# Two layers on one core: how the last sparsification's steps are spread among the closing products' additions

## Chip, core and metric

The kernel runs on one core of a Trainium2 chip. The metric is the device time of one execution in microseconds (us). Of three runs before the change the median is 1851.51 us (1851.51 to 1860.42).

## What is computed

The reference is a model of two layers on 2 x 1024 rows of 512 numbers in float32. Layer 0 is a scan branch with a small MLP beside a gated feed-forward network with a Hadamard transform; layer 1 is attention beside a gated feed-forward network whose hidden values are thinned: of each group of four, only the two of greatest magnitude stay. The part that matters here is the last one:

```
def _sparsify_2to4(h):
    g = h.reshape(B, S, I // 4, 4)
    a = jnp.abs(g)
    _, idx = jax.lax.top_k(a, 2)
    pos = jnp.arange(4)
    mask = (pos == idx[..., 0:1]) | (pos == idx[..., 1:2])
    return (g * mask).reshape(B, S, I)
h = silu(x @ w_gate) * (x @ w_up)          # 512 -> 2048
return _sparsify_2to4(h) @ w_down          # 2048 -> 512
...
x = x + attention(xn) + ffn(xn)
```

## The kernel before, in words

The engines work through one program in four stages: layer 0, attention, then layer 1's feed-forward network in the pool `c`. That last stage is what this study is about. It has 16 units: two pairs of row blocks (512 rows each), four groups of 512 hidden columns, two halves of a group. One unit makes 2 x 128 hidden columns for two row blocks in `gate_up`, with the matrix products of L179 by a Strassen-like scheme of seven products in place of eight. Two units fill `hs[n]`, the hidden values of group n (n from 0 to 7): 128 partitions, four members of each group of four, two row blocks i, 512 rows.

Each group is then thinned and multiplied by its rows of the down projection:

- `sparsify(n, half)` (L1385 to L1414) is a generator with twelve steps for one half of the rows (256 of each block). Step 1 is the absolute value on ScalarE (L1399, into `ab`); the other eleven are on VectorE: the smaller and larger of pairs (L1400, L1404), comparisons (L1402, L1403, L1406, L1407), the sums that turn them into a count of wins (L1408 to L1410), and two products of a mask with `h`, in place (L1414). Its buffers `ab`, `lo`, `first`, `both` and `way` exist once, so the second half's absolute value must wait until the first half has read `ab` for the last time (L1407). `some_steps(n, half, count)` runs the next `count` steps.
- `down_by_seven` (L246) makes the down projection of a half in seven products of 128 x 256 (L297), which it adds to the residual `x1` on VectorE (L310), or leaves to GpSimd (L315). Its products lie in two PSUM banks in turn; a product may begin on a bank only when the one before has been read from it.
- `row_down(n, i, j)` (L1449) makes 128 rows of the down projection directly: four matmul calls of 128 x 512 (L1454), which the profile counts as eight instructions, then an addition to the residual on VectorE (L1459), and for the last group of a pair of blocks the store of these rows by SyncE (L1462). It takes its bank from three pairs in turn.

While a unit's gate-and-up products run, hooks inside `gate_up` insert steps of the group before. Behind the last unit no gate-and-up products are left. What stands there is the list `tail`: the remaining products of group 6, first half (five of L297, with GpSimd's addition), the four `row_down` of group 6's second half, the thinning of group 7 and its eight `row_down`. The list is built by hand before the loop and then run through; `in_program_order(start2)` fixes the order on TensorE, VectorE, ScalarE and GpSimd as it is issued. Each engine works through its own queue in that order, and semaphores hold an instruction until what it reads or overwrites is ready.

Before the change the list interleaves as follows: the first half's absolute value; then, for each of the five products of group 6, a `row_down` of group 6 and one step, the product and one step (the fifth product has no `row_down` ahead of it); then two more steps (the two L1414 of the first half) and the second half's absolute value; then four `row_down` of group 7's first half, with 3, 3, 3 and 2 steps of the second half behind their additions; then the four `row_down` of the second half. A step behind a product stands on VectorE's queue behind that product's addition.

Of the kernel before, what the change touches and what calls it, by code (L numbers as in the profile page):

```python
# [35 lines left out]
def two_layers(ctx: ExitStack, tc: tile.TileContext, t: dict, out: bass.AP):  # L36
# [307 lines left out]
    with tc.tile_pool(name="a", bufs=1) as a:  # L344
# [386 lines left out]
        def down_weights(n, m):  # L731
# [16 lines left out]
        hidden_first, hidden_last, down, products_of = down_by_seven(  # L748
            a, h0, td, quarters_w, lambda n: n // (NU // 2) * 2, in_place=True
        )  # L750
# [35 lines left out]
        for q, n in enumerate(((0, 2), (0, 4), (1, 2), (1, 4))):  # L786
            put0(*n, fwht_rows, q)
            for m in range(4):
                n, at = (0, (4, 5, 6, 6)[m]) if q == 0 else divmod(4 * q + 3 + m, 7)
# [11 lines left out]
        for base in (0, NU):  # L801
            i, d = 2 * base // NU, base + (1 if base else 3)
# [88 lines left out]
        n, second_half = NU - 1, list(products_of(NU - 1, 1))  # L891
# [14 lines left out]
    with tc.tile_pool(name="b", bufs=1, reuse_waits="tile") as b:  # L906
# [304 lines left out]
        for u in range(len(units)):  # L1211

            for half in range(2):
                n = per * u - ahead + (3, 11)[half]
# [11 lines left out]
            for j in range(2):  # L1226
                n = per * u + 8 * j + 7
# [93 lines left out]
        n = len(second)  # L1321
# [14 lines left out]
    with tc.tile_pool(name="c", bufs=1, reuse_waits="tile") as c_:  # L1336
# [81 lines left out]
        def some_steps(n, half, count):  # L1418
# [5 lines left out]
        hidden_first, hidden_last, down, products_of = down_by_seven(  # L1424
            c_, hs, td, quarters_w, lambda n: 2 * units[2 * n][0]
        )
# [9 lines left out]
        between1, tail = {}, []  # L1436
# [5 lines left out]
        def sequence(n, half):  # L1442

            for step in products_of(n, half):
                yield step
                if step[0] == down and step[3] > 4:
                    yield store, n, half, step[3] - 5
# [16 lines left out]
        for n in range(groups - 1):  # L1464
# [8 lines left out]
            for half, at in enumerate(((8, 11),) if end else (range(4, 11), range(11, 18))):  # L1473
                steps = list(sequence(n, half))
# [11 lines left out]
                put1(u, 10, hidden_last, n, 1)  # L1486


        n = groups - 1
        rows = [(row_down, n - 1, i, j) for j in (2, 3) for i in range(2)]  # L1490
        behind_last, tail = tail, [(some_steps, n, 0, 1)]
        for what in behind_last:
            if what[0] == down:
                if rows:
                    tail += [rows.pop(0), (some_steps, n, 0, 1)]
                tail += [what, (some_steps, n, 0, 1)]
            else:
                tail.append(what)
        tail += [(some_steps, n, 0, 2), (some_steps, n, 1, 1)]
        for half in range(2):  # L1500
            for j in (2 * half, 2 * half + 1):
                for i in range(2):
                    tail.append((row_down, n, i, j))
                    if half == 0:
                        tail.append((some_steps, n, 1, (3, 3, 3, 2)[2 * j + i]))

        tt, next_tt, second = None, None, None
        s_of = {}
# [117 lines left out]
```

## Time and profile before

| What | us |
|---|---|
| median of three runs | 1851.51 |
| the profiled execution's own time | 1851.87 |
| its span, first to last instruction | 1850.1 |
| TensorE (PE) busy | 1794.7 (97%) |
| VectorE (DVE) busy | 1124.7 (61%) |
| GpSimd (POOL) busy | 819.6 (44%) |
| ScalarE (ACT) busy | 478.5 (26%) |
| mean granted clock of TensorE | 0.996 |

In the profile PE is TensorE's matrix work and PEld its weight loads, which overlap it. L1454 is line 1454 of the kernel. "PE dr L1454 x8" are eight instructions that write tile `dr`; "DVE h L1414" is VectorE's step that writes `h`. "A <- B" means that A waited for B. The granted clock is the share of full speed that TensorE was given. All times within the span are counted from its first instruction. The last gate-and-up product ends at 1786.4 us; the tail is what follows, some 64 us.

How VectorE's queue stands in a part of the tail before (start, length, engine, line, instruction; in brackets the idle time ahead and what ended it):

```profile
1806.91 0.69 DVE L1459 TENSOR_TENSOR x<-x,dr 128x512 f32<-128x512 f32 x1 [2.15 <-PE dr L1454]
1807.52 0.42 DVE L1408 TENSOR_TENSOR way<-both 128x512 bf16<-128x512 bf16 x1
1808.71 0.69 DVE L310 TENSOR_TENSOR x<-x,d 128x512 f32<-128x512 f32 x1 [0.77 <-PE d L297]
1809.31 0.68 DVE L1409 TENSOR_TENSOR first<-first,way 128x1024 bf16<-128x1024 bf16 x1
```

### The profile page before, as it was taken

What the parts mean: (1) busy time and instruction counts of PE and PEld (TensorE: products, weight loads), DVE (VectorE), ACT (ScalarE), POOL (GpSimd) and SP (SyncE); (2) the same over time, 40 slices, a digit from 0 to 9 for tenths busy, and PEclk for the clock granted to TensorE, in tenths of its full rate; (3) what the DMA queues carried; (4) which work ended last, traced back from release to release, by engine and by line L of the source; (5) the groups of instructions that cost most, each with busy time, mean ns of one, the idle gap of its engine ahead of it and who ended that gap; (6) DMA issues with size and microseconds to landing.
All of it is one profiled execution on the core that took longest, in us unless ns stands there. A gap on an engine that the chain in (4) does not pass through costs nothing.

```text
span 1850.1 us, 18897 instructions
## 1 busy us (share of the span) xinstructions
PE 1794.7 (97%) x7348; PEld 916.4 (50%) x7348; DVE 1124.7 (61%) x1464; ACT 478.5 (26%) x683; POOL 819.6 (44%) x711
## 2 busy tenths in 40 slices
PE   7999999999999999999999999999999999999998
PEld 4446566555555564333333333333455555555553
DVE  3685444556544438566666566752867778668654
ACT  2322222222221102334343443412212212211210
POOL 4335364256542222467666766623243343334300
PEclk9999999999999999999999999999999999999999
DMA  6121111011101100000001000011011112201101
GB/s 228 35 80 34 35 35 46 23 46 35 35 23 34 35 18 12 1 12 13 12 1 35 12 13 1 24 46 42 27 57 34 46 32 72 80 23 57 34 1 46
DMA packets 29465, 68.12 MB, mean 37 GB/s; under 512 B 3392, under 2 KB 11584, under 8 KB 27840
## 3 DMA queue, kind: packets, MB, share of 16 engines
q1 hardware_dynamic: 28656, 66.61, 11.1%
q8 instruction: 59, 0.97, 0.2%
q10 hardware_dynamic: 720, 0.30, 0.1%
q14 instruction: 30, 0.25, 0.0%
HBM read 62.70 MB, written 4.19 MB: 36 GB/s over the span
## 4 chain that ended last, share of the span: by engine, by line
PE 87%; DVE 5%; POOL 3%; ACT 2%; issue 2%; DMA 0%; SPq 0%; ACTq 0%; POOLq 0%; DVEq 0%
PE p_a L179 20%; PE p_c L179 19%; PE d L297 19%; PE pq L990 6%; PE m L1042 4%; PE s L1095 4%; PE o L1137 3%; PE po L990 3%; PE pv L990 3%; PE dr L1454 2%; POOL acc L1145 2%; PE w L1157 1%; DVE tops L1050 1%; PE pp L579 1%; PE s L1101 1%
## 5 line engine op out<-in xcount | busy, mean ns | idle before, releaser
L315 POOL TENSOR_TENSOR x<-x,de 128x512 f32<-128x512 f32 x87 | 125.4, 1456 | 297.3 <-DVE x L310 162.5
L1145 POOL TENSOR_TENSOR acc<-acc,pt 128x1024 f32<-128x1024 f32 (+3 forms) x138 | 233.6, 1717 | 0.0
L1050 DVE TENSOR_REDUCE tops<-m 128x2 f32<-128x1024 f32 (+2 forms) x192 | 180.8, 955 | 49.1 <-PE m L1042 44.6
L310 DVE TENSOR_TENSOR x<-x,d 128x512 f32<-128x512 f32 x145 | 99.2, 684 | 151.5 <-PE d L297 150.5
L1112 ACT ACTIVATE pt<-s 128x1024 f32<-128x1024 f32 (+3 forms) x160 | 115.1, 766 | 180.1 <-PE s L1101 166.9
L297 PE MATMUL d<-td,h 128*128 128x256 f32 x592 | 139.9, 380 | 2.2 <-DVE h L272 2.2
L297 PEld LDWEIGHTS d<-td,h 128*128 128x128 f32 x592 | 112.2, 190 | 46.2 <-issue 29.2
L990 PE MATMUL pq<-xt,wqk 128*128 128x512 f32 x256 | 124.5, 614 | 0.8 <-ACT qk L1006 0.8
L179 PE MATMUL p_a<-t_a,s_a 128*128 128x512 f32 x256 | 116.9, 600 | 2.0 <-DVE t_a L156 2.0
L179 PE MATMUL p_c<-xt,s_c 128*128 128x512 f32 x256 | 115.2, 593 | 2.5 <-DVE e_c L224 1.4
L179 PE MATMUL p_a<-xt,w 128*128 128x512 f32 x256 | 116.8, 599 | 0.7 <-ACT xt L136 0.7
L179 PE MATMUL p_a<-xt,s_a 128*128 128x512 f32 x256 | 116.6, 598 | 0.0
L179 PE MATMUL p_c<-xt,gu 128*128 128x512 f32 x256 | 114.9, 592 | 0.0
L179 PE MATMUL p_c<-t_c,s_c 128*128 128x512 f32 x256 | 114.6, 592 | 0.0
L1049 DVE TENSOR_TENSOR m<-m,mask 128x256 f32<-128x256 f32 x128 | 54.7, 427 | 97.3 <-PE m L1042 92.7
L1042 PE MATMUL m<-qk,qk 32*128 32x512 f32 (+3 forms) x768 | 107.2, 533 | 3.7 <-ACT acc L1112 3.0
L1095 PE MATMUL s<-qk,qk 32*128 32x512 f32 (+3 forms) x768 | 93.5, 532 | 3.1 <-ACT pt L1112 2.2
L172 POOL TENSOR_TENSOR s_c<-gu,s_c 128x512 f32<-128x512 f32 x16 | 20.4, 1275 | 134.2 <-PE p_c L179 134.2
L1117 POOL TENSOR_SCALAR_AFFINE_SELECT pt<-pt 128x256 f32<-128x256 f32 x112 | 48.3, 448 | 69.5 <-ACT pt L1112 68.9
L990 PEld LDWEIGHTS pq<-xt,wqk 128*128 128x128 f32 x256 | 44.2, 189 | 65.9 <-issue 61.8
L179 PEld LDWEIGHTS p_a<-xt,s_a 128*128 128x128 f32 x256 | 47.2, 190 | 57.1 <-issue 56.7
L179 PEld LDWEIGHTS p_c<-xt,s_c 128*128 128x128 f32 x256 | 48.5, 190 | 54.2 <-issue 52.9
(240 smaller groups left out, 3044.6 us busy)
## 6 DMA issues: line engine op xcount, KB each, us to landing
w<-in_W SPq DMA_DIRECT2D x32, 512.0 KB, 3.6
gu<-in_gu SPq DMA_DIRECT2D x32, 512.0 KB, 3.5
wd<-in_down SPq DMA_DIRECT2D x8, 1024.0 KB, 4.8
x<-in_x SPq DMA_DIRECT2D x16, 256.0 KB, 4.3
w2h<-in_W2q SPq DMA_DIRECT2D x4, 1024.0 KB, 11.5
xr<-in_x SPq DMA_DIRECT2D x16, 256.0 KB, 2.7
wqk<-in_WqkvT SPq DMA_DIRECT2D x16, 256.0 KB, 3.1
out_x<-x SPq DMA_DIRECT2D x16, 256.0 KB, 2.0
```

Source lines behind the costliest of these rows:

```text
L179: nc.tensor.matmul(pair[:, m, :], a[:, m, k, :], x[:, k, :], start=start and k == 0, stop=stop and k == 1, skip_group_check=True,)
L297: nc.tensor.matmul(out_[:, j, :], lhs[:, q, j * P : (j + 1) * P], rhs[:, q], start=m in (0, 1, 3, 4) and j == q == 0, stop=j == q == 1, sk ...
L310: nc.vector.tensor_add(r, r, out_)
L315: nc.gpsimd.tensor_add(r, r, u2[half])
L990: nc.tensor.matmul(got[0], lhs(k), rhs(k), start=(k == 0), stop=(k == KC - 1))
L1042: nc.tensor.matmul(pair[h // 2][:, h % 2, :e], q[rows, qt * P : (qt + 1) * P], k[rows, c * 512 : c * 512 + e], start=True, stop=True,)
L1049: nc.vector.tensor_add(d, d, mask.unsqueeze(1).to_broadcast([P, 2, P]))
L1050: nc.vector.tensor_reduce(out=tops[u][:, c, qt, 2 * p : 2 * p + 2], in_=pair[p][:, :, :e], axis=mybir.AxisListType.X, op=ALU.max,)
L1095: nc.tensor.matmul(pair[h // 2][:, h % 2, s:], k[rows, kt * P : (kt + 1) * P], q[rows, cols], start=True, stop=False,)
L1112: nc.scalar.activation(pt[:, :, s:], pair[p][:, :, s:], AF.Exp, scale=1.0 / math.sqrt(HD))
L1137: nc.tensor.matmul(po[rows, s:], v[:, rows], pts[h // 2][:, h % 2, s:], start=(kt == 0), stop=last, tile_position=(0, h * HD),)
L1145: eng.tensor_add(acc[:, :, s:], acc[:, :, s:], pt[:, :, s:])
```

## The change

It replaces the one-step interleaving by a written-out list. `steps` has twelve entries, each a tuple of (half, count); `go_on` takes the next entry and appends those steps to the tail. One entry is taken before the first product, one behind each of the nine products of group 6 (four `row_down`, five of L297), and one behind each of group 7's first two `row_down`. On VectorE that gives, by addition: first half's L1400 ahead of the first addition; then behind the additions in turn L1402; L1403 and L1404; L1406 and L1407; L1408 to L1410; both L1414; the second half's L1400; L1402; L1403 and L1404; L1406 and L1407; and behind the first two additions of group 7 L1408 and L1409; L1410 and both L1414. On ScalarE the second half's absolute value is issued behind the first half's L1410. No instruction is added or dropped, and the order on TensorE, GpSimd and SyncE is the same.

```diff
         n = groups - 1
         rows = [(row_down, n - 1, i, j) for j in (2, 3) for i in range(2)]
-        behind_last, tail = tail, [(some_steps, n, 0, 1)]
+        steps = [
+            ((0, 2),), ((0, 1),), ((0, 2),), ((0, 2),), ((0, 3), (1, 1)), ((0, 2),), ((1, 1),),
+            ((1, 1),), ((1, 2),), ((1, 2),), ((1, 2),), ((1, 3),),
+        ]
+
+        def go_on():
+            for half, count in steps.pop(0) if steps else ():
+                tail.append((some_steps, n, half, count))
+
+        behind_last, tail = tail, []
+        go_on()
         for what in behind_last:
+            if what[0] == down and rows:
+                tail.append(rows.pop(0))
+                go_on()
+            tail.append(what)
             if what[0] == down:
-                if rows:
-                    tail += [rows.pop(0), (some_steps, n, 0, 1)]
-                tail += [what, (some_steps, n, 0, 1)]
-            else:
-                tail.append(what)
-        tail += [(some_steps, n, 0, 2), (some_steps, n, 1, 1)]
+                go_on()
         for half in range(2):
             for j in (2 * half, 2 * half + 1):
                 for i in range(2):
                     tail.append((row_down, n, i, j))
-                    if half == 0:
-                        tail.append((some_steps, n, 1, (3, 3, 3, 2)[2 * j + i]))
+                    go_on()
```

## The prediction

> **What bounds the kernel now.** I read the page first, then the chain of waits in order of time for the last 85 us (the change touches only what follows the last gate-and-up unit of layer 1), then busy time and granted clock by stretches there, then VectorE's own timeline, and last the order in which the changed kernel puts the instructions on each engine. By the page TensorE is busy 97% of the span and carries 87% of the chain that ended last, so a gain must come from a place where TensorE stands still or runs slowly. The end of the chain (start in us, length, what):
>
> ```profile
> 1803.44 3.43 PE dr L1454 x8
> 1806.87 3.47 PE d L297 x16
> 1810.34 0.03 issue
> 1810.37 0.02 DVEq L310
> 1810.39 0.04 issue
> 1810.44 0.69 DVE x L310
> 1811.12 0.60 DVE first L1410
> 1811.72 1.15 DVE h L1414
> 1812.87 0.04 issue
> 1812.91 15.71 PE dr L1454 x32
> 1828.63 0.02 issue
> 1828.65 0.69 DVE x L1459
> 1829.34 1.15 DVE h L1414
> 1830.48 0.04 issue
> 1830.53 15.71 PE dr L1454 x32
> 1846.24 0.02 issue
> 1846.26 0.69 DVE x L1459
> ```
>
> TensorE leaves the chain twice, each time for VectorE's last steps of a sparsification: from 1810.34 to 1812.91 (2.57 us) and from 1828.63 to 1830.53 (1.90). The first row shows what one row product, eight matrix instructions, costs undisturbed: 3.43. Thirty-two should then take 13.72, and both groups take 15.71. The granted clock shows most of the other 1.99 (stretch, its length, busy time and count of PE, PEld, DVE, ACT and POOL, clock, DMA share, GB/s):
>
> ```profile
> 1812.90:1814.00 1.10, 1.08 (x3) 0.61 (x4) 1.09 (x1) 0.00 (x0) 0.00 (x0) 0.95 0.00 0
> 1814.00:1817.20 3.20, 3.20 (x5) 1.20 (x4) 0.00 (x0) 0.00 (x0) 0.00 (x0) 0.50 0.00 0
> 1817.20:1828.60 11.40, 11.40 (x27) 4.78 (x25) 9.34 (x12) 0.00 (x0) 0.00 (x0) 1.00 0.18 69
> 1830.50:1834.40 3.90, 3.87 (x5) 1.65 (x6) 1.11 (x1) 0.00 (x0) 0.00 (x0) 0.56 0.13 43
> 1834.40:1846.30 11.90, 11.82 (x28) 4.94 (x26) 2.10 (x4) 0.00 (x0) 0.00 (x0) 1.00 0.18 66
> ```
>
> After each stop TensorE runs some 3.3 us at half clock. That loses 0.06 + 1.60 = 1.66 behind the first stop and 3.90 x 0.44 = 1.72 behind the second. The rest, about 0.27, is the restart: the first row product behind the 1.31 us gap at 1787.69 takes 3.70 where 3.43 is usual, with the clock at 1.00.
>
> **The change part by part.** No instruction is added or taken away on any engine, and TensorE's order is the same. What moves is the place of VectorE's 22 sparsification instructions among the additions, and ScalarE's second absolute value.
>
> What goes: both stops with what hangs on them. From 1810.34 to 1846.24 is 35.90 us; eight row products at 3.43 are 27.46 with nothing in between. The difference is 8.44: 4.47 of standing, 3.98 of restart and half clock. For it TensorE must find everything ready eight times, so I replayed VectorE in the new order. It takes its queue in order. The pitches are from this trace's neighbouring starts: an addition 0.60 (1818.35 to 1818.95), each of L1400 to L1404 1.14 (1818.95, 1820.09, 1821.22), L1406 and L1407 0.60, L1408 0.45, L1409 and L1410 0.60, the two L1414 together 2.35. An addition can't start before its product ends, by the present chain at 1791.39, 1793.12, 1796.55, 1798.28, 1801.71, 1803.44, 1806.87, 1808.60 and 1810.34.
>
> First half: L1400 starts at 1791.0, when ScalarE's first absolute value ends (1790.97), ahead of the first addition, which moves from 1791.43 to 1792.15. Then L1402 1792.75, addition 1793.9, L1403 1794.5, L1404 1795.7, addition 1796.9, L1406 1797.5, L1407 1798.1, addition 1798.7, L1408 1799.3, L1409, L1410 to 1800.9, addition 1801.75, both L1414 from 1802.35 to 1804.7. The half is thin at 1804.7, where TensorE needs it at 1810.34: 5.6 us early, not 2.57 late.
>
> Second half: its absolute value reuses the first half's buffer, so it waits for L1407, as now (L1407 then at 1804.08, the ACTIVATE at 1804.86). It moves to 1798.9 and ends at 1800.8 on a ScalarE that has nothing else to do. Addition 1804.7, L1400 1805.3, addition 1806.9, L1402 1807.5, addition 1808.7, L1403 1809.3, L1404 1810.6, addition 1811.7, L1406 and L1407 to 1813.5. The row product of 1810.34 ends at 1813.77: addition 1813.8, L1408 and L1409 to 1815.5. The next ends at 1817.2: addition, L1410 1817.8, both L1414 from 1818.4 to 1820.8. TensorE comes to the second half at 1810.34 + 4 x 3.43 = 1824.07. It is 3.3 us early.
>
> The price is that additions come later, and each frees a bank. The tightest: L310 of the sixth of these nine products now stands behind the L1414 pair and ends at 1805.4 (before: 1804.2). The ninth product reuses its bank and would start at 1808.60, which leaves 3.2 us. The eighth needs L310 of the fourth, done by 1799.4, at 1806.87. The other banks have over 5 us. GpSimd's last addition of the residual waits for that same L310 and goes from 1804.24 to about 1805.4; its reader is the addition at 1817.2. SyncE's eight stores still follow their additions one by one 3.43 us apart, and the last still has 1846.95 to 1850.1, 3.15 us, behind it. So I price all moves at nothing, covered by TensorE's own products. If the cover failed, a stall would cost its idle time, 0.27 of restart and up to 1.7 of half clock. In sum VectorE has 22 steps and 11 additions, 26.1 us, in the 29.8 us from 1791.0 to 1820.8: full, but ahead. What is late next is nothing of VectorE's; TensorE runs through.
>
> One rule speaks against part of the gain. The Trainium skill (TensorE: Matmul & The Clock Gate, "Why this matters for your kernels") has the matrix clock drop only after a gap of some 3 us, one idle window of about 3.4 (its part on the clock gate). By that rule neither stop would cost clock, and the change would bring only the standing and two restarts, 4.47 + 0.54 = 5.0, for 1846.5. The rows above decide against the rule: after 2.57 and after 1.90 us the clock was 0.50. But gaps of 1.81 us at 1209.2 and 1.31 at 1786.4 left it at 1.00. A window that runs on its own, as the same page describes, fits the rows if less than a whole window of idling is enough: the slow stretches begin about 1.0 and 0.5 us after the restarts, and last about as long as its window. Then what a gap costs depends on where it falls, and a kernel without gaps over 1.3 us there has nothing to lose. I take the measured 1.99 each.
>
> The sum against the profiled execution: span 1850.1 - 8.44 = 1841.66; 1.77 us lie outside of it (1851.87 - 1850.1), so 1843.4. The median, 1851.51, is 0.36 under the profiled time, too little for it to have escaped either half-clock stretch: 1851.51 - 8.44 = 1843.1. That is 0.46% less, just inside the 0.5% that a measurement of this kernel can tell from no change.
>
> **The rivals.** *One wait comes back.* VectorE is full 26.1 of 29.8 us; if the additions that are now behind two or three steps pile up, TensorE could stop at the ninth product or at the second half, and half the gain would be lost: 1.90 + 1.99 = 3.9, so 1847.0. Against it: after the row product that ends at 1817.2 only 3.6 us of VectorE's work (0.60 + 0.60 + 2.35) stands between, and TensorE needs 6.87 to arrive. Chance 0.09.
>
> *Only the standing goes.* If the clock drops once or twice anyway, as its window may fall on the 1.31 us gap at 1786.4, the time is 1844.8 to 1846.5. Against it is that the gap is left unchanged, and this trace shows 1.00 behind it. Chance 0.05.
>
> *Slower: the FIFO blocks TensorE.* The place is L310 behind the L1414 pair, which holds the bank of the ninth product, and the second half's own steps, queued behind that. It decides from the point at which VectorE's work from 1801.75 on takes 3.2 us longer than its rows, and the kernel is slower when the new stalls exceed 8.44: two of 2.3 us idle with 1.99 each. That needs VectorE's 26.1 us to become some 35, by a third. The same instructions ran at the same pitches beside TensorE earlier in this trace (the L1414 pair 2.35 at 1769.24). The worst that I can build is 1856 to 1862. Chance 0.03.
>
> *No effect.* The stores, not TensorE, could set the end. But each lands about 2 us after its issue, with 3.43 between them. Chance 0.03, 1851.5.
>
> **How the numbers follow.** The likeliest, 0.80, is 1843.1; its own range is 1842.0 to 1844.5, from the 0.36 between profile and median and half a us of replay. One of the three runs shown lies 8.9 us above the other two, and the profile cannot explain that; should the median of after fall on such a run, it would be near 1852. The range goes from 1841.5 to 1848.0, over the two partial cases; the slower case, no effect and most of that scatter stay out. Faster by over 0.5% means under 1842.25, 0.85 us below my number: 0.16, for scatter and an undersized clock term. Slower by over 0.5%: 0.04. Within: 0.80.
>
> **What would show it.** Right: in the chain of the changed kernel, sixty-four instructions of L1454 in one piece of 27.5 us from about 1810.3 with the clock at 1.00; no wait of L1454 for L1414; the first half's L1414 pair at about 1802.4, the second's at about 1818.4; the last L1459 at about 1837.8; the stretch before 1790 unchanged. Wrong: a TensorE gap before the ninth product or before the fifth of the last eight row products, L1414 of the second half ending after 1824, or half clock behind a gap that I call harmless.

## The result, and the profile after

| | before | after |
|---|---|---|
| median us (lowest to highest, runs) | 1857.08 (1851.51 to 1860.42, 8) | 1847.94 (1847.09 to 1850.59, 8) |
| ratio after / before | | 0.9958, 95% interval 0.9946 to 0.997 |
| profiled execution, us | 1851.87 | 1850.59 |
| its span, us | 1850.1 | 1848.8 |
| tail: end of the last gate-and-up product to end of the last row product | 1786.38 to 1846.24 = 59.86 | 1793.53 to 1844.94 = 51.41 |

The kernel is faster by 0.42%, 7.8 us (5.6 to 10.0) of 1857.1. The two profiled executions differ by 1.3 us only. The table's last row shows why: the tail is 8.45 us shorter, but it starts 7.15 us later, though nothing ahead of it was changed.

The end of the chain that ended last, after (start, length, what):

```profile
1810.58 3.43 PE dr L1454 x8
1814.01 3.45 PE d L297 x16
1817.46 27.48 PE dr L1454 x64
1844.94 0.02 issue
1844.97 0.69 DVE x L1459
```

VectorE no longer comes in between: all eight row products are one piece of 27.48 us. Busy time and clock by stretches of the tail (length, then PE, PEld, DVE, ACT, POOL, then the clock):

```profile
1793.50:1797.00 3.50, 2.19 (x6) 1.06 (x6) 1.91 (x2) 1.43 (x2) 0.00 (x0) 1.00 0.00 0
1797.00:1817.40 20.40, 20.40 (x69) 12.83 (x68) 17.98 (x22) 3.02 (x2) 2.19 (x1) 1.00 0.00 0
1817.40:1845.00 27.60, 27.53 (x65) 11.88 (x63) 11.95 (x18) 0.00 (x0) 0.00 (x0) 1.00 0.18 67
```

From 1797 on TensorE is busy throughout at full clock. VectorE, busy 17.98 of the 20.40 us, is where the work went. Four instructions of its timeline show the margins:

```profile
1809.49 2.35 DVE L1414 SCALAR_TENSOR_TENSOR h<-first,h 128x1024 f32<-128x1024 bf16 x2
1811.77 0.68 DVE L310 TENSOR_TENSOR x<-x,d 128x512 f32<-128x512 f32 x1
...
1814.05 0.69 DVE L1459 TENSOR_TENSOR x<-x,dr 128x512 f32<-128x512 f32 x1 [0.47 <-PE dr L1454]
...
1825.65 2.35 DVE L1414 SCALAR_TENSOR_TENSOR h<-first,h 128x1024 f32<-128x1024 bf16 x2
```

The first half is thin at 1811.8, 5.6 us ahead of TensorE, and the L310 whose lateness I called tightest is done at 1812.5, 3.3 us before the ninth product starts on its bank (1815.7 by the chain). The second half is done at 1828.0; TensorE comes to it at 1817.46 + 13.74 = 1831.2, 3.2 us later.

Most of the 7.15 us are in this profile too, in four stretches far ahead of the change:

```profile
75.50:79.00 3.50, 3.50 (x7) 1.81 (x7) 3.46 (x4) 0.00 (x0) 0.00 (x0) 0.53 0.43 136
809.50:813.00 3.50, 3.50 (x19) 1.65 (x16) 1.55 (x4) 1.88 (x4) 3.50 (x6) 0.55 0.00 0
1215.30:1218.70 3.40, 3.40 (x10) 1.17 (x4) 2.00 (x4) 0.00 (x0) 1.39 (x2) 0.52 1.00 419
1321.30:1324.70 3.40, 3.40 (x7) 2.44 (x8) 3.30 (x5) 2.37 (x3) 0.00 (x0) 0.51 0.00 0
```

In each of them the clock is near 0.5 for about 3.4 us; by the clock that is 1.7 us lost apiece, 6.8 in all. The first profile of before had none between 40 and 1800 us, although its gaps there were the same: 1.81 us ahead of 1210.97, for one, and then

```profile
1210.90:1215.00 4.10, 4.03 (x23) 1.33 (x23) 3.24 (x5) 0.58 (x1) 1.99 (x4) 1.00 0.96 402
```

### The profile page after: what moved, and what is told of

It is laid out like the page before. It is cut to its first block, busy times and chain, and to the rows that moved or that the text cites. A ratio compares the mean times of both kernels' runs of the same rounds, so it can differ in the third digit from the quotient of the medians.

```text
span 1848.8 us, 18896 instructions
## 1 busy us (share of the span) xinstructions
PE 1798.2 (97%) x7348; PEld 918.6 (50%) x7348; DVE 1127.4 (61%) x1464; ACT 478.5 (26%) x683; POOL 821.1 (44%) x711
## 4 chain that ended last, share of the span: by engine, by line
PE 88%; DVE 5%; POOL 2%; ACT 2%; issue 2%; DMA 1%; ACTq 0%; POOLq 0%; DVEq 0%
PE p_a L179 20%; PE p_c L179 19%; PE d L297 19%; PE pq L990 6%; PE m L1042 4%; PE s L1095 4%; PE o L1137 3%; PE po L990 3%; PE pv L990 3%; PE dr L1454 2%; POOL acc L1145 2%; PE w L1157 1%; DVE tops L1050 1%; PE pp L579 1%; PE s L1101 1%
## 5 line engine op out<-in xcount | busy, mean ns | idle before, releaser
L310 DVE TENSOR_TENSOR x<-x,d 128x512 f32<-128x512 f32 x145 | 99.3, 685 | 149.8 <-PE d L297 148.6
L297 PE MATMUL d<-td,h 128*128 128x256 f32 x592 | 139.9, 380 | 2.2 <-DVE h L272 2.2
L297 PEld LDWEIGHTS d<-td,h 128*128 128x128 f32 x592 | 112.2, 190 | 46.2 <-issue 29.0
```

The costliest lines, as they stand in the source:

```text
L297: nc.tensor.matmul(out_[:, j, :], lhs[:, q, j * P : (j + 1) * P], rhs[:, q], start=m in (0, 1, 3, 4) and j == q == 0, stop=j == q == 1, sk ...
L310: nc.vector.tensor_add(r, r, out_)
```

## Experiments

Theory: each stop in the tail cost its standing, a restart and half clock; the change removes both; and what the clock's gate (whatever sets the granted clock to full or half) takes elsewhere falls differently from execution to execution, which moved the base of the sum. Rivals: the half clock had another cause than the stops; the early begin of the second half is what pays; the first profile of before was typical and something else is slower.

| kernel | tail starts | tail us | half clock seen between 60 and 1780 | median us (runs) | ratio to before |
|---|---|---|---|---|---|
| before | 1786.38 | 59.86 | none | 1857.08 (8) | |
| before_again | 1791.33 | 59.84 | 75 (twice as long), 1184, 1214 | 1856.71 (1) | |
| after | 1793.53 | 51.41 | 75, 809, 1215, 1321 | 1847.94 (8) | 0.9958 (0.9946 to 0.997) |
| after_again | 1789.82 | 51.42 | 75, 1319 | 1846.83 (5) | 0.9947 (0.9934 to 0.9961) |
| first_half_only | 1789.16 | 53.59 | 75, 1212 | 1851.7 (11) | 0.9979 (0.9971 to 0.9988) |
| second_half_late | 1792.18 | 51.55 | 75 (twice as long), 1213, 1320 | 1847.49 (6) | 0.9959 (0.9948 to 0.9971) |
| before_filled | 1789.44 | 56.45 | 75, 1212 | 1852.6 (22) | 0.9981 (0.9974 to 0.9987) |
| seven_first | 1791.78 | 49.85 | 75, 809, 1184, 1215 | 1846.44 (6) | 0.9953 (0.9941 to 0.9965) |
| seven_first_filled | 1792.83 | 49.84 | 75, 1320 | 1850.46 (9) | 0.9972 (0.9961 to 0.9983) |
| one_fill | 1788.22 | 49.85 | 1055, 1183 | 1844.61 (5) | 0.9938 (0.9926 to 0.9951) |

**first_half_only.** The first half as in the change, the second as before:

```diff
-            ((0, 2),), ((0, 1),), ((0, 2),), ((0, 2),), ((0, 3), (1, 1)), ((0, 2),), ((1, 1),),
-            ((1, 1),), ((1, 2),), ((1, 2),), ((1, 2),), ((1, 3),),
+            ((0, 2),), ((0, 1),), ((0, 2),), ((0, 2),), ((0, 3),), ((0, 2),), (), (), (),
+            ((1, 1),), ((1, 3),), ((1, 3),), ((1, 3),), ((1, 2),),
```

> The first half's steps are spread as in the change, the second half's begin only behind group 7's first row product, 3, 3, 3 and 2 as before. I measure the tail, from the end of the last gate-and-up product to the end of the last row product: 59.86 us in the kernel before, 51.41 in the changed one. My theory: the first stop goes and the second stays at about 1.9 us, so the tail is 59.86 - 4.56 = 55.3 us if the clock drops behind the second stop, 53.6 if it does not; in time about 4 us below the kernel before. The rival that the early begin of the second half is what pays expects the first stop to move to the second half and a tail of 57 or more.

Its chain:

```profile
1813.09 13.75 PE dr L1454 x32
1826.84 0.02 issue
1826.86 0.69 DVE x L1459
1827.55 1.15 DVE h L1414
1828.69 0.04 issue
1828.74 14.02 PE dr L1454 x32
```

The first stop is gone and the second stands, 1.90 us, as the theory said. Its products take 14.02 and not 15.71: the clock behind the stop stayed at 1.00. The same 1.90 us cost clock in before and nothing here. In time the kernel is 3.9 us (2.2 to 5.4) below the kernel before, as expected, and not the 6.27 by which this profile's tail is shorter: the profiled execution is the fastest of the eleven, so this stop may well cost clock in most of them. One profile doesn't show it.

**second_half_late.** The same first half; the second half's absolute value is issued ahead of group 7's first row product, then six steps behind it and five behind the next:

```diff
+            ((0, 2),), ((0, 1),), ((0, 2),), ((0, 2),), ((0, 3),), ((0, 2),), (), (), (),
+            ((1, 1),), ((1, 6),), ((1, 5),),
```

> The first half's steps are spread as in the change; the second half's VectorE steps begin only behind group 7's first row product, six behind it and five behind the next. My theory: VectorE's 9.8 us of steps fit between 1814.4 and 1824.0 of the replay, with 0.1 to 0.2 us to spare, so no stop stands in the trace, the tail is 51.4 to 51.7 us, and the time is that of the changed kernel. The rival that the second half must be begun among group 6's products expects a stop of 1 us or more ahead of the second half's row products and a tail of 52.5 to 55.

```profile
1812.66 3.45 PE d L297 x16
1816.11 27.62 PE dr L1454 x64
1843.73 0.02 issue
```

No stop, a tail 0.14 us longer than the changed kernel's, and a ratio within its interval. The second half's early begin among group 6's products carries no more than those 0.14 us by itself; it buys margin. What matters is that each half is thin before TensorE comes to it.

**before_filled.** The kernel before, with products in its stops that nobody reads:

```diff
+        def idle_fill(count):
+            bank = ps_wide(f"fill_{count}")[:, 0, :]
+            for r in range(count):
+                nc.tensor.matmul(bank, ident, wd[groups - 1][:, r, :], start=True, stop=True)
+
         for half in range(2):
+            tail.append((idle_fill, 3 - half))
```

> The kernel before, with matrix products into a bank that nobody reads in its two stops: three of 128x512 ahead of group 7's first row product and two ahead of its fifth. The steps stay where they were, so what was waited for comes no sooner. My theory, that a stop costs its idle time, 0.27 of restart and 1.7 of half clock: the clock is 1.00 through the tail, the tail is 59.86 - 2 x 1.98 = 55.9 us, and the time is some 4 us below the kernel before. The rival, that only the standing costs and the half clock has another cause, expects a tail of 59.9 and half clock in the tail as before.

```profile
1813.37 2.58 PE fill L1503 x6
1815.94 0.01 issue
1815.96 14.02 PE dr L1454 x32
1829.97 0.02 issue
1830.00 0.69 DVE x L1459
1830.69 1.14 DVE h L1414
1831.83 0.04 issue
1831.87 14.02 PE dr L1454 x32
```

Each half still starts when VectorE is done, but takes 14.02: the clock was 1.00 throughout the tail. The restart stayed (14.02 against 13.74 to 13.75 without a wait), which I had counted as saved; so 56.45 and not 55.9. This run isolates the half clock of the tail: 59.86 - 56.45 = 3.41 us. By the times it is 3.5 (2.4 to 4.8), which agrees with both stops paying in most executions of before, as they did in both its profiles.

**seven_first.** The order of the two products is turned round:

```diff
-            if what[0] == down and rows:
-                tail.append(rows.pop(0))
-                go_on()
             tail.append(what)
             if what[0] == down:
                 go_on()
+                if rows:
+                    tail.append(rows.pop(0))
+                    go_on()
```

> The changed kernel with each product of 128x256 ahead of its row product in place of behind it. The product needs no bank that VectorE still holds, so it covers the 1.31 us gap at the tail's start. My theory: the gap and its restart go, the tail is 51.41 - 1.31 - 0.27 = 49.8 us, no stop elsewhere, and the time is 1.6 us below the changed kernel. The rival, that VectorE has no room for another order, expects a stop of TensorE ahead of the ninth product or of the second half, and a tail of 51.4 or more.

```profile
1784.91 6.87 PE p_c L179 x16
1791.78 1.73 PE d L297 x8
1793.51 3.43 PE dr L1454 x8
```

The gap at the tail's start is gone, 49.85 as forecast. In time that doesn't show: by the medians it is 1.5 us under the changed kernel's first series and 0.4 under its second (after_again), and the intervals of the ratios overlap.

**gaps_alone.** A kernel of its own: bursts of products, a gap of chosen length by a chain of VectorE operations, the next burst. It leaves out the model and writes a block of the input to all of the output.

> A kernel of its own that leaves out the model and writes one block of the input to all of the output: 144 bursts of matrix products of 9.5 to 12.5 us at full clock, each followed by a gap in which TensorE waits for a chain of VectorE operations on the burst's result. Nine lengths of gap from about 0.9 to 4.5 us, sixteen of each, the bursts' lengths changed so that the gaps fall at different places. My theory, a window of some 3.4 us that runs on its own and that must be idle for about half: no gap under about 1.3 us costs clock, gaps of 1.8 to 2.6 us cost it in a share of the cases that grows with the gap, gaps over 3.4 us always; a burst that pays is longer by about 1.7 us. The rival, that the clock drops only after a whole idle window, expects nothing under 3.4 us to pay. The other rival, that the gap's length alone decides, expects a sharp border between 1.81 and 1.90 us.

```profile
839.80 2.04 PE L34 MATMUL g<-x,c 128*128 128x512 f32 x2 [2.33 <-DVE c L45]
...
853.81 1.13 PE L34 MATMUL g<-x,c 128*128 128x512 f32 x2 [2.24 <-DVE c L45]
```

Two neighbouring gaps of 2.3 us: behind the first the two instructions take 2.04, behind the second 1.13. I compared each burst with the shortest of its own make; one that lost over 0.5 us counts as paid:

| gap, us | 0.79 | 1.24 to 1.34 | 1.51 to 1.60 | 1.97 to 2.06 | 2.24 to 2.33 | 2.69 to 2.79 | 2.96 to 3.06 | 3.69 to 3.78 | 4.41 to 4.51 |
|---|---|---|---|---|---|---|---|---|---|
| paid | 0 of 16 | 0 of 16 | 0 of 16 | 8 of 16 | 9 of 16 | 11 of 16 | 12 of 16 | 14 of 16 | 15 of 15 |

A payment under 3.4 us of gap was nearly always 1.4 to 1.7 us. Both rivals fall: gaps far below 3.4 us pay, and one length pays now and then. Only "over 3.4 always" was too strong (14 of 16 at 3.7).

The trace also holds the time of each change of the clock, and that settles what decides. In the twelve profiles there are 247 stretches of one clock from change to change, and each is a whole multiple of 3.413 us, to within 0.003: the clock is set anew by a window that runs on its own. I laid these windows over gaps_alone and added up TensorE's idle time in each (40 to 2099 us). Of those at full clock all 69 with 1.97 us or more are followed by a window of half clock, and none of the 447 with 1.96 or less. So a gap pays when enough of it falls into one window: one of 3.78 us, cut into 1.94 and 1.84 by a window's border, did not. A window that is itself at half clock was followed by another when 0.62 us of it were idle (17 windows; none of 69 with 0.56 or less).

The border is not the same in the model's kernels, where other products stand around the gaps. Around 1320 us two gaps, 0.29 and 1.5 us, are followed by half clock where both lie in one window (1.80 us idle in all: after, after_again, second_half_late), and not where the window holds 1.68 or less. The tail's second stop left 1.92 us idle in its window in before, before_again and first_half_only alike; the first two paid, the third did not. What decides so near the border stays open.

**before_again.** The kernel before, unchanged, profiled once more.

> The kernel before, unchanged, profiled once more. My theory: its profiled execution of 1851.87 us was one that paid for half clock in the tail alone, while most executions pay at one to five further places ahead of it, 1.4 to 1.7 us each, since the gate's window falls differently on the same gaps. So this profile shows half clock somewhere between 60 and 1330 us, above all behind the 1.81 us gap at about 1212, a tail's start between 1788 and 1795 instead of 1786.4, a tail between 56.4 and 59.9, and a time of 1854 to 1860. The rival, that the first profile is what this kernel does and the later runs are slower for another reason, expects the tail's start at 1786.4 again and the clock at 1.00 everywhere but at the start and in the tail.

```profile
75.00:78.00 3.00, 3.00 (x6) 1.45 (x7) 2.97 (x3) 0.00 (x0) 0.00 (x0) 0.50 0.41 137
1183.90:1187.00 3.10, 3.10 (x16) 1.01 (x20) 1.28 (x3) 0.79 (x2) 1.59 (x5) 0.50 0.00 0
...
1214.30:1219.00 4.70, 4.69 (x21) 1.79 (x22) 2.72 (x5) 0.00 (x0) 1.93 (x3) 0.64 0.96 404
```

The same program, 1856.71 us: the tail is the same to 0.02 us, and starts 4.95 us later behind three such stretches. The first profile was the rare one: of the 65 timed runs of before seven lie under 1852, and two of the three runs that I had are among these seven.

The gate's windows show why one gap costs clock in one execution and not in the next. Here are the windows around the 1.81 us gap, first in the first profile of before, then in before_again (stretch, its length, then busy time of PE, PEld, DVE, ACT and POOL, and the clock):

```profile
1209.74:1213.15 3.41, 2.18 (x11) 0.97 (x12) 3.11 (x5) 0.13 (x1) 3.15 (x5) 1.00 0.85 291
1213.15:1216.57 3.42, 3.42 (x16) 1.22 (x15) 1.03 (x3) 0.58 (x1) 0.00 (x0) 1.00 0.77 323
...
1211.15:1214.57 3.42, 1.61 (x19) 0.51 (x17) 3.12 (x4) 0.66 (x2) 3.25 (x4) 1.00 0.27 48
1214.57:1217.98 3.41, 3.41 (x11) 1.36 (x8) 2.27 (x4) 0.00 (x0) 1.66 (x3) 0.50 1.01 423
```

In the first a border cuts the gap, and 1.23 us of it fall into the window shown; in the second all 1.81 us lie in one window, and the next has half clock. In the eight profiles that have this gap unfilled it lies whole in one window six times, and these six paid; it is cut twice (before, after_again), and these two did not.

**seven_first_filled** and **one_fill.** Filling of the same kind far ahead of the tail, at two places and then at one:

```diff
+                if n == len(second) - 1:
+                    bank = ps_wide("fill_a")[:, 0, :]
+                    for r in range(2):
+                        nc.tensor.matmul(bank, ident, wout[:, r, :], start=True, stop=True)
                 gather(*behind)
...
+        def idle_fill():
+            bank = ps_pair("fill_b", turns % 3)[:, 0, :]
+            for r in range(2):
+                nc.tensor.matmul(bank, ident, wd[0][:, r, :], start=True, stop=True)
+
+        put1(2, 4, idle_fill)
```

> The kernel with each 128x256 product ahead of its row product, and two matrix products of 128x512 into a bank that nobody reads in each of two gaps far ahead of the tail: the 1.81 us gap at about 1212 and the 1.8 us around 1320. My theory: the clock stays at 1.00 behind both, no work comes sooner, the tail is 49.8 us as without the filling, and the median falls by 1.5 to 2.5 us below that of seven_first (1846.44). Half clock at 70 to 80 us, where TensorE is never idle but runs products of 8 and 16 columns, remains. The rival, that these places don't set the scatter of the times, expects no change of the median, or a rise by up to 1 us for the added products.

```profile
1318.37 3.68 PE L1471 MATMUL fill_b<-wd,ident 128*128 128x512 f32 x4 [3.64 <-DVE e_c L204]
```

The second filling failed by its place: it waited for a bank that VectorE had not yet read, stood 3.64 us where gaps of 0.29 and 1.5 were to be covered, and the clock halved behind it. The median is 4 us above that of seven_first. The first did its work, and one_fill keeps it alone:

> As seven_first_filled, with the filling at about 1212 us alone. The filling at 1320 is left out: it waited 3.64 us for a bank that a busy VectorE still held, and so made a longer stop than the one it was to cover. My theory: the clock is 1.00 behind 1212, the tail is 49.8 us, and the median lies 1.0 to 1.7 us under that of seven_first (1846.44), since in eight of nine profiles so far TensorE paid there. The rival, that a gap which is filled only moves the gate's window on to the next gap, expects half clock at another place and a median within 0.5 us of 1846.44.

The count in that text is wrong: TensorE had paid there in six of the seven profiles without the filling that there were by then.

```profile
1208.00:1212.40 4.40, 4.40 (x28) 1.69 (x20) 4.40 (x4) 1.62 (x4) 2.59 (x2) 1.00 0.16 24
1212.40:1217.00 4.60, 4.60 (x25) 1.50 (x24) 3.32 (x6) 0.59 (x1) 2.32 (x4) 1.00 0.91 374
```

The gap is filled and the clock stays at 1.00 there. The median, 1844.61, is 1.8 us under seven_first and 2.2 under after_again beside it on the chip, the lowest of this study; but its interval against before overlaps after_again's, so a gain from this filling is not shown. Half clock at 1055, seen in no other profile, is what the rival expects, but one profile cannot decide it, since the windows fall differently in each execution.

**after_again.** The changed kernel, profiled and timed once more:

> The changed kernel, unchanged, profiled and timed beside one_fill on the same chip. My theory: a tail of 51.4 us with the clock at 1.00 in it, half clock at two to four places between 60 and 1330 us, a median of 1847 to 1848.5, and a ratio to the kernel before of 0.995 to 0.9965. The rival, that the gain comes from which executions were caught, expects a ratio whose interval reaches 0.998.

The tail is 51.42 and the clock halves at two places ahead of it, as expected. Median and ratio, 1846.83 and 0.9947 (0.9934 to 0.9961), lie just under what I had named; the first series had 0.9958. The 1.81 us gap at 1212 did not pay this time, since a window's border cuts it.

**small_products.** At 75 us TensorE does not stand still: it runs products of 8 and 16 columns. A last kernel of its own has bursts of large products with small ones between, and no gap; it too leaves out the model and writes a block of the input.

> A kernel of its own that leaves out the model and writes one block of the input to all of the output: bursts of ten products of 128x512 (and up to seven of 128x256 so that they fall at different places), each followed without a gap by about 3.4 us of small products: thirteen of 8 columns, thirteen of 64, sixteen of 128 or eight of 256, sixteen times each. If the clock's gate counts what streams through the array and not that an instruction runs, as half clock at 75 us without an idle TensorE suggests, the 8-column case pays half clock in most of its sixteen bursts and the 256-column case never. The rival, that only standing counts, expects clock 1.00 behind all four, and half clock at 75 us to have another cause.

```profile
13.70:16.50 2.80, 2.80 (x27) 2.78 (x25) 0.00 (x0) 0.00 (x0) 1.00 0.49 184
17.10:20.40 3.30, 3.30 (x6) 1.22 (x4) 0.31 (x1) 0.00 (x0) 0.50 0.00 0
...
310.00:313.40 3.40, 3.40 (x13) 2.13 (x12) 0.00 (x0) 0.00 (x0) 1.00 0.00 0
```

The first row is the 8-column products, the second what follows them, the third what follows 64-column ones. Half clock stands eleven times in the 8-column part of sixteen bursts (once for two windows) and never in the other three. They were shorter than the 3.4 us I had meant: both 8 and 64 columns took 2.8. Eleven of sixteen is also what idle gaps of 2.69 to 2.79 us gave in gaps_alone, so here the 8-column products count about as little as standing still.

## Why the prediction was right and wrong

**Right: the tail.** Forecast 8.44 us, measured 8.45; eight row products in one piece of 27.48 (27.46); the margins of 5.6 us for the first half, 3.3 for the ninth product's bank and 3.2 for the second half, where the replay had 5.6, 3.2 and 3.3; no new wait. The restart and the half clock, priced at 3.98, hold: before_filled shows 3.41 for the clock by itself. Taking the row against the rule was right as well; gaps_alone shows payments from 1.97 us on. So was the guess of a window that runs on its own.

**Wrong: the base.** The step that failed is "The median, 1851.51, is 0.36 under the profiled time, too little for it to have escaped either half-clock stretch: 1851.51 - 8.44 = 1843.1". The difference was right and the number it was taken from was not. The median before is 1856.4 to 1857.5 in four series of runs. With 1857.08 the same sum gives 1848.6; 1847.94 was measured. The term that I had at nothing is half clock ahead of the tail: the profiled execution had none and before_again three stretches, 4.95 us. That two of the first three runs were such rare ones was bad luck; to take them for the rule was the mistake. I had both clues in the text, a window that runs on its own and one run 8.9 us above the others, and wrote of the latter that the profile cannot explain it. The range, up to 1848.0, holds the time only at its edge, and by luck: its width was meant for other cases.

**Wrong: what can be told.** The second step that failed is "just inside the 0.5% that a measurement of this kernel can tell from no change". I had no number for these 0.5%, and gave 0.80 to "within 0.5%" as if that were no difference. Eight runs on each side give the ratio to 0.12% either way, so the 0.42% are a gain clear of the scatter: the intervals 0.9946 to 0.997 and 0.9934 to 0.9961 stay below 1.

**Half right: the gap rule of the sum.** I wrote that 1.81 and 1.31 us at 1209.2 and 1786.4 "left it at 1.00" as a property of those gaps. The 1.81 us gap paid in six of the eight profiles that have it, after among them, and so two of my own signs came out against me: half clock behind a gap that I called harmless, and a stretch before 1790 that did not stay unchanged. Whether a gap from about 1.8 to 3.8 us pays is a matter of where the window's border cuts it. Single gaps up to 1.6 us paid in none of 48 cases of gaps_alone, but 0.29 and 1.5 us in one window paid at 1320.

**The rivals.** None of the waits came back, no stall was made, and the stores did not set the end: it follows the start of the last addition by 3.8 us before and after.

## What to carry to other kernels

Before a difference is taken from a time, ask whether the profiled execution is a typical one: compare the stretches of half clock ahead of the change, not only the span, and if few runs are known keep their spread in the base. A stop of TensorE of about 2 us or more can cost 1.7 us on top, and short stops close together add up, so steps that feed it are best spread until each is ready some us early. An order that lets a product go first whose bank is free took another 1.56 us off the tail here. Products that fill a stop keep the clock, but only if they wait for nothing themselves.

## What the runs showed of the hardware

Not foreseen in the prediction: products of 8 columns count for the clock about as idling does. After 2.8 us of them, with TensorE busy all the time, the clock was 0.50 for 3.4 us in eleven places, while the same time with 64 columns left it at 1.00 each time. The model's kernels have such places too: at 809, 1055 and 1184 us windows with only 0.85 to 1.31 us of idling were followed by half clock, among products with 32 or 3 rows (32*128 and 3*128 in the trace); that these count less as well is likely and was not tested. And the same program has a different number of half-clock stretches between 60 and 1780 us from one execution to the next: none and three in the two profiles of before, which differ by 4.84 us (1851.87 and 1856.71), four and two in those of after.
